# Layer 2's written-out block loop: stores and casts in later slots, refinement factors on ScalarE a block ahead, affine passes on GpSimd

## The chip, the core and the metric

The kernel runs on one core of a Trainium2 chip. A core has TensorE (PE, matrix products, transposes), VectorE (DVE), ScalarE (ACT) and GpSimd (POOL) for elementwise work, and SyncE (SP), which here only issues transfers. ScalarE issues transfers too, in its own instruction order. Each engine takes its instructions strictly as they stand in its queue, and waits on semaphores of the others. The metric is the device time of one execution in microseconds (us). The kernel before took 4350.38 us (median of three runs, 4346.45 to 4351.04).

## What is computed

Four graph layers over 4096 nodes with 256 features, each followed by a residual sum and a layernorm. Layers 0, 1 and 3 use the given 4096 x 4096 adjacency. The change lies in layer 2, which takes two steps of attention and diffusion:

```python
for n in range(2):
    A = top_p_attention(Xa, W1, W2, W3)      # rows of softmax, the largest kept up to 0.9 of the sum
    Xf = R @ Xf                              # R: adjacency plus identity, rows divided by their sum
    Xa = A @ Xa
    Z = Z + Xf @ U1[n].T + Xa @ U2[n].T
h = X + Z
x = layernorm(X + layernorm(h) * ln_g + ln_b)
```

The top-p cut of a row needs no full sort in the kernel. It guesses a cut, lists the largest elements below the guess, and finds the exact cut among these. In step 1 the guess is first made better by one Newton-like refinement.

## The kernel before, in words

Rows are worked in 32 blocks of 128 (NB = 32). For each step of layer 2 there is a preparation (keys, the first scores, a projection of all blocks) and then a loop over blocks b = 0..30, written out by hand with eight slots s = 0..7 in each block. Inside that loop the orders on PE, ACT, DVE and POOL are exactly the order in which the code calls them (`manual_schedule`). SyncE is not in that list: a planner orders its transfers, and may place one earlier in the queue than the slot in which the code asks for it.

In block b the slots hold, side by side, work for several blocks:

- **gather** (L1262): eight groups of products of the transposed, masked attention rows of block b with X, into the single buffer `ps_a`. Each group uses an `aT` that **turn** (L1253 transposes, L1255 ScalarE copy) made two slots earlier; the turns in slots 6 and 7 are already those of block b+1.
- **diffusion** (L175 load, L178 products) of block b+1, into the single buffer `ps_r`. It takes eight adjacency pieces of 256 KB from three `adj_piece` buffers, so piece p4 is loaded into the buffer of p1, and so on. In step 0 the slots hold 0,0,2,1,2,1,2,0 pieces, in step 1 0,0,2,1,2,2,1,0: in both, p4 is the first piece of slot 4.
- **scores** (L921, exponential L925) of block b+2 in slots 0 and 1.
- **guessed** for block b+2 on ScalarE in slots 2 to 7: a chain of 128x1 operations (helper `fma`, L934) around four 128x2048 passes (L1015). In slot 7 it ends with `c2`.
- **nucleus** for block b+1 on VectorE in slots 0 to 5: in slot 0 the cut `hi` (in step 1 after a full pass `S2` over the row, L941, and a chain of small operations, part of it on GpSimd, L1048 to L1053), in slots 1 and 2 a masked pass over half a row (L1070) and eight MAX8 (L1074) each, in slots 3 and 4 small operations, in slot 5 the mask passes over `e` (L1125).
- at the start of the block, **store** (step 0, L1358) or **closing** (step 1, L1365) of block b-1: ScalarE copies `ps_a` out as `h`. Only then may the next gather write `ps_a`.
- **diffused** (L1292): two VectorE passes that add the two halves of `ps_r` to `xb`. **base** (L1284/L1286) loads the next `xb` through SyncE, into one of two buffers.
- step 0: **keep** (slot 1): ScalarE casts `xb` (L126), VectorE subtracts (L127); the transfer out follows in slot 5.
- step 1: the rest of **closing**: first layernorm statistics in slot 1 (L85, L86 on VectorE, L88, L89 on GpSimd), the two affine passes on VectorE (L1370, L1371) and the second layernorm in slot 2 (L96 on GpSimd), the transfer of `h` out, issued by ScalarE, in slot 3 (L1374). **ahead3** turns and projects the `h` of two blocks before.

Of the kernel before, what the change touches and what calls it, by code (L numbers as in the profile page):

```python
# [23 lines left out]
P = 128  # L24
# [31 lines left out]
class Net:  # L56
# [684 lines left out]
    def layer2(self):  # L741
# [3 lines left out]
        with ExitStack() as ctx:  # L745
# [184 lines left out]
            def small(name, n=1, bufs=2):  # L930
                return work.tile([P, n], F32, name=name, bufs=bufs)
# [5 lines left out]
            def evaluate(name, e, c, bufs=2):  # L937
# [12 lines left out]
            def scores(b, q):  # L950

                zp = small("zp", HALF // 512)
                yield from product(q, es[b % 3][:, :N], sums=zp)
                zj = small("zj", HALF // 512)
                nc.scalar.activation(zj, zp, AF.Identity, accum_out=Zs[:, b:b + 1])

            def guessed(step, b):
# [26 lines left out]
                w = small("w", bufs=3)  # L984
                thr = small("cutoff", bufs=3)
                far = small("far", bufs=3)
                few = small("few")

                def rest(k):
# [34 lines left out]
                c2 = small("c2", bufs=3)  # L1024
                fma(c2, S1, ri, w)
                return c1, c2, S1, ri, thr, far

            def nucleus(step, b, c1, c2, S1, ri, thr, far):
# [9 lines left out]
                low, hi = small("low"), small("hi")  # L1038
                if step == 0:
                    nc.vector.tensor_scalar_mul(low, c1, 0.3)  # L1040
                    nc.vector.tensor_scalar(hi, c2, low, far, op0=ALU.max, op1=ALU.mult)
                else:
                    c, ic, gw, sq, d = (small(n) for n in ("c3", "ic", "gw", "sq", "d"))
# [7 lines left out]
                    nc.gpsimd.tensor_mul(gw, gw, ic)  # L1051
                    nc.gpsimd.tensor_scalar(sq, sq, 400.0, ri, op0=ALU.add, op1=ALU.mult)
                    nc.gpsimd.tensor_scalar_mul(low, c, 0.3)  # L1053
# [38 lines left out]
                nc.vector.tensor_copy(above[:, b:b + 1], bef[:, 0:1])  # L1092
# [35 lines left out]
            def mend(step, e, r):  # L1128
# [3 lines left out]
                with tc.If(nc.values_load(row[:, NB:], min_val=0, max_val=1) == 0):  # L1132
                    with tc.For_i(0, NB - 1, 1) as b:
                        with tc.If(nc.values_load(row[:, at(b)], min_val=0, max_val=1) == 0):
                            e2, Z = exact_scores(b)
                            r2 = exact_nucleus(e2, Z)
                            if step == 1:
                                xb = diffused(b, whole(diffusion(step, b)), base(step, b))
# [40 lines left out]
            def exact_scores(b, e=None):  # L1179
# [6 lines left out]
                nb = work.tile([P, 1], F32, name="nb")  # L1186
                nc.vector.tensor_reduce(nb, e, AX.X, ALU.max)
                nc.vector.tensor_scalar(nb, nb, -1.0, LOG_LIFT, op0=ALU.mult, op1=ALU.add)
                Z = work.tile([P, 1], F32, name="Z")
# [3 lines left out]
            def exact_nucleus(e, Z):  # L1193
# [7 lines left out]
                thr = work.tile([P, 1], F32, name="thr")  # L1201
# [4 lines left out]
                for bit in range(FREE_BITS - 1, -1, -1):  # L1206
                    S = work.tile([P, 1], F32, name="S")
                    nc.vector.scalar_tensor_tensor(junk, e, cand.bitcast(F32), e, op0=ALU.is_ge, op1=ALU.mult,
                                                   accum_out=S)
                    ok = work.tile([P, 1], I32, name="ok")  # L1210
# [8 lines left out]
                S = work.tile([P, 1], F32, name="S")  # L1219
                nc.vector.scalar_tensor_tensor(junk, e, tf, e, op0=ALU.is_gt, op1=ALU.mult, accum_out=S)  # L1220

                lim = work.tile([P, 2], F32, name="lim")
# [4 lines left out]
                sums = work.tile([P, N // CH], F32, name="sums")  # L1227
                before = -1.0
                for c in range(N // CH):
# [5 lines left out]
                    last = work.tile([P, 1], F32, name="last")  # L1235
# [6 lines left out]
                r = work.tile([P, 1], F32, name="r")  # L1242
# [118 lines left out]
            def closing(b, pa, r, xb):  # L1361
# [9 lines left out]
                nc.vector.scalar_tensor_tensor(hb, hb, rstd, xb[:, 1], op0=ALU.mult, op1=ALU.add)  # L1371
# [21 lines left out]
            for step in range(2):  # L1393
# [29 lines left out]
                with tc.manual_schedule(engines={ET.PE, ET.Activation, ET.DVE, ET.Pool}):  # L1423
                    for b in range(NB - 1):
# [6 lines left out]
                        for s in range(8):  # L1431
                            if s == 0:
# [6 lines left out]
                                bases[b] = diffused(b, pr, xb)  # L1439
# [25 lines left out]
                            if s == 5 and kept:  # L1465
# [25 lines left out]
                xb = diffused(b, pr, xb)  # L1491
# [127 lines left out]
```

## Time and profile before

| what | value |
|---|---|
| median of three runs | 4350.38 us |
| profiled execution | 4347.05 us, span of its instructions 4345.4 us |
| granted TensorE clock, mean | 0.975 |
| busy over the span | PE 92%, DVE 71%, ACT 61%, POOL 18% |
| loop of step 0 | from about 1820 to 2750 us; ScalarE's `h` (L1358) starts every 29.97 to 30.02 us |
| loop of step 1 | from about 2957 to 4045 us; ScalarE's `h` (L1365) starts every 34.9 to 35.4 us, mostly 34.98 |
| step 0, 2200 to 2300 us | PE 94.86, DVE 81.83, ACT 78.04, POOL 0.58 us busy in 100; clock 1.00 |
| step 1, 3250 to 3350 us | PE 90.67, DVE 90.00, ACT 68.98, POOL 34.52 us busy in 100; clock 0.98 |

The span is the time from the first to the last instruction; the profiled execution's own time is 1.65 us more. A timeline row gives the start, the length, engine, line, operation, and in brackets the idle time of that engine just before, with what ended it. A row of the waits gives who waited for whom, the total, the number of times and the longest. "PEld" is TensorE's weight load, which overlaps the products. "SPq" rows are transfers that SyncE issues. Times in text are from the start of the span.

### The profile page before, as it was taken

The page shows a single profiled execution, that of the slowest core. Times are in us where ns is not written, and L with a number is a line of the kernel's source. Part 1 is how long each engine was busy: PE and PEld are TensorE (multiplying, and loading weights), DVE is VectorE, ACT ScalarE, POOL GpSimd, SP SyncE. Part 2 cuts the span into 40 slices and gives each one's busy share as a digit, 9 for nine tenths or more (in the row PEclk, how much of TensorE's full clock was granted, in tenths as well). Part 3 has the DMA queues.
Part 4 walks back from the last instruction along what each step waited for, and adds up shares of the span by engine and source line. Part 5 has one row for each costly group of instructions (what it writes and reads, how often), then busy time and mean ns, then how long its engine had stood idle before and what let it go on. Part 6 is the DMA issues. An engine that isn't in the chain of part 4 may idle for free. (4 is left out here: it accounts for less than half of the span.)

```text
span 4345.4 us, 68954 instructions
## 1 busy us (share of the span) xinstructions
PE 3989.1 (92%) x25177; PEld 3402.9 (78%) x25177; DVE 3106.8 (71%) x7186; ACT 2651.1 (61%) x4695; POOL 796.9 (18%) x970
## 2 busy tenths in 40 slices
PE   7999989999997997899999999778999999999699
PEld 6899989999996884488888888636777777777587
DVE  7642349999994545477878778447999998999354
ACT  5533359999894224487877777245666666665232
POOL 0111111112430111100000000023333333333011
PEclk9999999999999999999999999999999999999899
DMA  4765562342223983322323323622222222222541
GB/s 126 228 200 176 179 233 80 103 156 80 65 71 137 361 313 77 114 88 92 97 89 95 94 87 97 203 65 90 89 88 87 84 84 85 88 85 86 188 132 48
DMA packets 301835, 537.03 MB, mean 124 GB/s; under 512 B 38310, under 2 KB 134310, under 8 KB 297382
## 3 DMA queue, kind: packets, MB, share of 16 engines
q1 hardware_dynamic: 209668, 379.80, 27.1%
q10 hardware_dynamic: 78946, 112.66, 7.5%
q0 software_dynamic: 12864, 39.99, 3.0%
q8 instruction: 203, 3.33, 0.3%
q14 instruction: 154, 1.26, 0.1%
HBM read 370.44 MB, written 161.87 MB: 123 GB/s over the span
## 5 line engine op out<-in xcount | busy, mean ns | idle before, releaser
L1262 PE MATMUL ps_a<-X,aT 128*128 128x256 f32 x4096 | 995.3, 387 | 88.4 <-ACT aT L1255 59.8
L1262 PEld LDWEIGHTS ps_a<-X,aT 128*128 128x128 f32 x4096 | 778.6, 193 | 237.4 <-ACT aT L1255 79.5
L299 PE MATMUL acc<-gm,gt 128*128 128x198 bf16 x8192 | 704.9, 249 | 25.8 <-issue 15.0
L299 PEld LDWEIGHTS <-gt 128*128 128x128 fp8e4 x8192 | 700.9, 97 | 29.9 <-issue 15.4
L291 ACT ACTIVATE sg<-lpb,nlc 128x1024 fp8e4<-128x1024 f32 x640 | 671.3, 1135 | 60.0 <-DVE gt L293 34.9
L178 PE MATMUL ps_r<-XD,adj_piece 128*128 128x512 f32 x2048 | 581.6, 418 | 5.9 <-DVE XD L127 4.5
L516 PE MATMUL pz<-src,ar 128*128 128x264 f32 x4096 | 509.7, 287 | 12.8 <-DVE ar L506 11.0
L516 PEld LDWEIGHTS pz<-src,ar 128*128 128x128 f32 x4096 | 506.7, 189 | 15.8 <-DVE ar L506 13.5
L1015 ACT ACTIVATE ja<-e,nc 128x2048 uint8<-128x2048 f32 x240 | 481.1, 2004 | 12.1 <-POOL h L96 8.8
L1255 ACT COPY aT<-ps_tp 128x512 f32<-128x512 f32 x512 | 296.3, 580 | 313.8 <-PE ps_tp L1253 293.7
L178 PEld LDWEIGHTS ps_r<-XD,adj_piece 128*128 128x128 f32 x2048 | 368.1, 191 | 86.2 <-issue 15.1
L1253 PE MATMUL ps_tp<-ident,e 128*128 128x128 f32 x2048 | 315.1, 278 | 60.2 <-DVE e L1125 44.1
L1253 PEld LDWEIGHTS ps_tp<-ident,e 128*128 128x128 f32 x2048 | 258.9, 144 | 126.9 <-issue 80.8
L1074 DVE MAX8 cand<-v 128x8 f32<-128x256 f32 x1024 | 347.2, 411 | 4.4
L1125 DVE SCALAR_TENSOR_TENSOR e<-e,edge 128x512 f32<-128x512 f32 x512 | 346.9, 750 | 2.2
L509 ACT ACTIVATE nb<-a 128x512 uint8<-128x512 f32 x256 | 156.4, 630 | 292.3 <-DMA a<-in_adjt_dram 280.4
L202 ACT ACTIVATE adj_piece<-na 128x1024 fp32r<-128x1024 fp8e4 x128 | 135.3, 1060 | 318.5 <-PE ps_adj L1525 91.9
L1070 DVE SCALAR_TENSOR_TENSOR v<-e,hi 128x2048 f32<-128x2048 f32 x128 | 299.0, 2336 | 1.2
L925 ACT ACTIVATE e<-ps_logit 128x1024 f32<-128x1024 f32 x256 | 259.8, 1022 | 42.3 <-PE ps_logit L921 27.6
L284 DVE TENSOR_SCALAR sg<-lpb,nlc 128x1024 fp8e4<-128x1024 f32 x384 | 282.7, 772 | 2.0
L921 PE MATMUL ps_logit<-kT,q 128*128 128x512 f32 x1024 | 276.5, 410 | 8.0 <-DVE kT L879 6.3
L88 POOL TENSOR_SCALAR ln_var<-ln_mv 128x1 f32<-128x1 f32 (+1 forms) x144 | 163.3, 1134 | 534.4 <-DVE ln_mv L86 497.0
(317 smaller groups left out, 5216.2 us busy)
## 6 DMA issues: line engine op xcount, KB each, us to landing
adj_piece<-adjs SPq DMA_DIRECT2D x512, 256.0 KB
a<-in_adjt_dram SPq DMA_DIRECT2D x256, 256.0 KB
adjs<-adj_piece SPq DMA_DIRECT2D x96, 512.0 KB
na<-nad SPq DMA_DIRECT2D x64, 512.0 KB
na<-nad ACTq DMA_DIRECT2D x32, 1024.0 KB
nad<-nb POOLq DMA_DIRECT2D x128, 128.0 KB, 3.3
lpb<-lpd POOLq DMA_DIRECT2D x32, 512.0 KB, 4.1
xfd<-part ACTq DMA_DIRECT2D x63, 256.0 KB
```

The costliest lines, as they stand in the source:

```text
L178: nc.tensor.matmul(ps, a[:, k, :], rhs(jc).rearrange("p s d -> p (s d)"), start=(jc == 0), stop=(jc == self.NB - 1))
L284: nc.vector.tensor_scalar(sg[:, k, :], lpb, nlc[:, jc, h:h + 1], 2.0 ** -5, op0=ALU.is_ge, op1=ALU.mult, saturate=False)
L291: nc.scalar.activation(sg[:, k, :], lpb, AF.Sign, scale=-1.0, bias=nlc[:, jc, h:h + 1], saturate=False)
L299: nc.tensor.matmul(acc[:, q, :6 * C1], gt[:, k, q * P:(q + 1) * P], gm[:, jc, hh, :], start=(jc == 0 and q % 2 == 0), stop=(jc == NB - 1 a ...
L516: nc.tensor.matmul(pz[q][:, t, :W], ar[:, q, k, :], src[:, jc, t, s], start=(jc == 0 and s == 0), stop=(jc == NB - 1 and s == 1))
L1015: nc.scalar.activation(ja, e[:, s * HALF:(s + 1) * HALF], f, bias=nc1, accum_out=fs[:, i + s:i + s + 1])
L1070: nc.vector.scalar_tensor_tensor(v, ec, hi, ec, op0=ALU.is_lt, op1=ALU.mult, accum_out=sb[:, s:s + 1])
L1074: nc.vector.max(cand[:, 8 * j:8 * j + 8], v[:, k * 256:(k + 1) * 256])
L1125: nc.vector.scalar_tensor_tensor(ec, ec, edge[:, j:j + 1], ec, op0=ALU.is_ge, op1=ALU.mult)
L1253: nc.tensor.transpose(pt[:, k * P:(k + 1) * P], e[:, jc * P:(jc + 1) * P], self.ident)
L1255: nc.scalar.copy(aT, pt)
L1262: nc.tensor.matmul(pa[:, :D], aT[:, k * P:(k + 1) * P], X[:, jc, :], start=(jc == 0), stop=(jc == NB - 1))
```

## The change

- `keep` (step 0): cast in slot 2, subtraction in slot 4, transfer in slot 6, in place of slots 1, 1 and 5.
- `diffused`: ScalarE scales the second half of `ps_r` into a new tile `dif` (one buffer), VectorE adds the first half to it in one pass, and GpSimd adds `dif` to `xb` after the first gather.
- `guessed` (step 1): what slot 0 of `nucleus` computed on VectorE and GpSimd (`c`, its reciprocal, `gw`, `sq`, the lower bound) is made by eleven ScalarE operations at the end of slot 7, a block ahead. The reciprocal is Ln and Exp. `w` is one ScalarE `fma` with `nthr`, not a multiplication and a GpSimd subtraction; `low` is made on ScalarE.
- `closing` (step 1): all of the first layernorm, with the affine multiplication and addition, on GpSimd in slot 1; the second layernorm in slot 3; the transfer of `h` in slot 7.
- `ahead3`'s transfers go from slot 5 to slot 6; the copy of `above` goes from VectorE to GpSimd.
- Most small tiles get one buffer in place of two; some per-block tiles two in place of three.

```diff
-            def small(name, n=1, bufs=2):
+            def small(name, n=1, bufs=1):
...
                     elif k == 1:
                         nc.scalar.mul(thr, Z, TOP_P)
-                        nc.scalar.mul(w, thr, ri)
-                        nc.gpsimd.tensor_sub(w, c1, w)
+                        nc.scalar.mul(nthr, Z, -TOP_P)
+                        fma(w, nthr, ri, c1)
+                        nc.scalar.mul(low, c1, 0.3)
...
                 fma(c2, S1, ri, w)
-                return c1, c2, S1, ri, thr, far
+                if step == 0:
+                    return c2, low, far, thr
+                c, gw, sq, lows = (small(n, bufs=2) for n in ("c3", "gw", "sq", "lows"))
+                ic = small("ic")
+                fma(c, low, -1.0, c2, AF.Relu)
+                fma(c, c, 1.0, low)
+                nc.scalar.activation(ic, c, AF.Ln)
+                nc.scalar.activation(ic, ic, AF.Exp, scale=-1.0)
+                fma(gw, S1, 1.0, nthr)
+                nc.scalar.mul(gw, gw, ic)
+                nc.scalar.activation(sq, gw, AF.Square)
+                nc.scalar.mul(gw, gw, ic)
+                fma(sq, sq, 1.0, cs[:, 11:12])
+                nc.scalar.mul(sq, sq, ri)
+                nc.scalar.mul(lows, c, 0.3)
+                return c, lows, far, thr, S1, gw, sq
...
                 if step == 0:
-                    nc.vector.tensor_scalar_mul(low, c1, 0.3)
-                    nc.vector.tensor_scalar(hi, c2, low, far, op0=ALU.max, op1=ALU.mult)
+                    nc.vector.tensor_scalar(hi, c, low, far, op0=ALU.max, op1=ALU.mult)
                 else:
-                    nc.vector.scalar_tensor_tensor(c, c1, 0.3, c2, op0=ALU.mult, op1=ALU.max)
-                    nc.vector.reciprocal(ic, c)
-                    nc.gpsimd.tensor_sub(gw, S1, thr)
-                    nc.gpsimd.tensor_mul(gw, gw, ic)
-                    nc.gpsimd.tensor_mul(sq, gw, gw)
-                    nc.gpsimd.tensor_mul(gw, gw, ic)
-                    nc.gpsimd.tensor_scalar(sq, sq, 400.0, ri, op0=ALU.add, op1=ALU.mult)
-                    nc.gpsimd.tensor_scalar_mul(low, c, 0.3)
                     S2 = evaluate("S2", e, c)
...
-                nc.vector.tensor_copy(above[:, b:b + 1], bef[:, 0:1])
+                nc.gpsimd.tensor_copy(above[:, b:b + 1], bef[:, 0:1])
...
             def diffused(b, pr, xb):
-                for part in (slice(0, D), slice(D, 2 * D)):
-                    nc.vector.scalar_tensor_tensor(xb[:, 0], pr[:, part], rdeg[:, at(b)], xb[:, 0],
-                                                   op0=ALU.mult, op1=ALU.add)
+                dif = work.tile([P, D], F32, name="dif", bufs=1)
+                nc.scalar.mul(dif, pr[:, D:], rdeg[:, at(b)])
+                nc.vector.scalar_tensor_tensor(dif, pr[:, :D], rdeg[:, at(b)], dif, op0=ALU.mult, op1=ALU.add)
+                yield
+                nc.gpsimd.tensor_add(xb[:, 0], xb[:, 0], dif)
                 return xb
...
-                self.split(part, xb[:, 0])
+                nc.scalar.copy(part[:, 0], xb[:, 0])
+                yield
+                nc.vector.tensor_sub(part[:, 1], xb[:, 0], part[:, 0].bitcast(F32))
                 yield
                 nc.scalar.dma_start(xfd[b], part.bitcast(F32))
...
                 nc.gpsimd.tensor_add(hb, hb, xb[:, 0])
                 yield
-                mv, rstd = self.moments(work, h)
+                self.layernorm(work, h, h, nc.gpsimd)
+                nc.gpsimd.tensor_mul(hb, hb, affine)
+                nc.gpsimd.tensor_add(hb, hb, xb[:, 1])
                 yield
-                nc.vector.scalar_tensor_tensor(hb, hb, mv[:, 0, 0:1], affine, op0=ALU.subtract, op1=ALU.mult)
-                nc.vector.scalar_tensor_tensor(hb, hb, rstd, xb[:, 1], op0=ALU.mult, op1=ALU.add)
                 self.layernorm(work, h, h, nc.gpsimd)
...
-                                bases[b] = diffused(b, pr, xb)
+                                difs = diffused(b, pr, xb)
+                                next(difs)
...
                             gather(pa, aTs.pop(0), s)
-                            if s in (1, 2, 3) and close:
+                            if s == 0:
+                                bases[b] = result(difs)
+                            if s in (1, 3, 7) and close:
                                 v = result(close)
-                                if s == 3:
+                                if s == 7:
                                     done[b - 1] = v
-                            if s == 1 and step == 0:
-                                kept = keep(b, bases.pop(b))
-                                next(kept)
+                            if step == 0:
+                                if s == 2:
+                                    kept = keep(b, bases.pop(b))
+                                if s in (2, 4, 6):
+                                    result(kept)
...
-                            if s == 5 and kept:
+                            if s == 6 and step == 1 and kept:
                                 whole(kept)
```

More of the change, by code (lines that the diff above doesn't have):

```diff
@@ L950, in scores @@
             def scores(b, q):
-                zp = small("zp", HALF // 512)
+                zp = small("zp", HALF // 512, bufs=2)
                 yield from product(q, es[b % 3][:, :N], sums=zp)
@@ L983, in guessed @@
                 ri = small("ri", bufs=3)
-                w = small("w", bufs=3)
+                w = small("w", bufs=2)
                 thr = small("cutoff", bufs=3)
+                nthr = small("nthr")
+                low = small("low", bufs=2)
                 far = small("far", bufs=3)
@@ L1200, in exact_nucleus @@
                 CH = 1024
-                thr = work.tile([P, 1], F32, name="thr")
+                thr = work.tile([P, 1], F32, name="thr", bufs=1)
                 nc.vector.tensor_scalar_mul(thr, Z, TOP_P)
@@ L1226, in exact_nucleus @@
                 nc.vector.tensor_scalar_mul(lim[:, 1:2], tf, -1.0)
-                sums = work.tile([P, N // CH], F32, name="sums")
+                sums = work.tile([P, N // CH], F32, name="sums", bufs=1)
                 before = -1.0
@@ L1234, in exact_nucleus @@
                     nc.vector.tensor_tensor_scan(cnt, ones.to_broadcast([P, CH]), eq, before, op0=ALU.mult, op1=ALU.add)
-                    last = work.tile([P, 1], F32, name="last")
+                    last = work.tile([P, 1], F32, name="last", bufs=1)
                     nc.vector.tensor_copy(last, cnt[:, CH - 1:CH])
@@ L1241, in exact_nucleus @@
                                                    accum_out=sums[:, c:c + 1])
-                r = work.tile([P, 1], F32, name="r")
+                r = work.tile([P, 1], F32, name="r", bufs=1)
                 nc.vector.tensor_reduce(r, sums, AX.X, ALU.add)
@@ L1490, in layer2 @@
                         finish(k, done.pop(k))
-                xb = diffused(b, pr, xb)
+                xb = whole(diffused(b, pr, xb))
                 if step == 0:
```

24 lines of the change are left out of this document (12 added, 12 removed).

## The prediction

> **What bounds the kernel now.** The change touches the two loops of layer 2, so I read the waits of each loop's window, then the instruction timeline of one steady block, then short stretches with busy time and clock.
>
> The waits of step 0's loop (1820 to 2780 us):
>
> ```profile
> DVE part L127 <- ACT part L126: 134.7, 30, 4.7
> PE ps_tp L1253 <- DVE e L1125: 38.5, 30, 1.3
> ```
>
> TensorE works through each 29.98 us block but for 1.28 us, when it waits for VectorE's first mask pass. VectorE is late because it stood 4.5 us behind ScalarE's cast. So TensorE alone would need 28.7 us.
>
> The waits of step 1's loop (2980 to 4050):
>
> ```profile
> POOL h L1366 <- ACT h L1365: 285.1, 31, 13.0
> ACT part L126 <- POOL h L96: 195.4, 25, 7.8
> ...
> DVE d L1055 <- POOL gw L1051: 45.8, 30, 1.6
> PEld ps_a L1262 <- ACT h L1365: 38.7, 29, 3.4
> ```
>
> VectorE's only real wait is 1.58 us: it bounds the 34.98 us block. ScalarE stands up to 7.8 us, and TensorE waits for it at each block's first gather.
>
> One block of step 1, rows of the timeline (all engines; rows between left out):
>
> ```profile
> 3301.13 0.47 ACT L1365 ACTIVATE h<-ps_a,inv 128x256 f32<-128x256 f32 x1
> ...
> 3301.68 4.45 POOL L1366 TENSOR_TENSOR h<-h,xb 128x256 f32<-128x256 f32 x1 [9.05 <-ACT h L1365]
> ...
> 3309.29 2.32 DVE L1070 SCALAR_TENSOR_TENSOR v<-e,hi 128x2048 f32<-128x2048 f32 x1
> 3309.30 1.27 SPq L175 DMA_DIRECT2D adj_piece<-adjs  x2
> 3309.46 2.23 POOL L88 TENSOR_SCALAR ln_var<-ln_mv 128x1 f32<-128x1 f32 x1 [1.65 <-DVE ln_mv L86]
> ...
> 3311.77 0.57 POOL L89 TENSOR_TENSOR ln_rstd<-ln_var,power 128x1 f32<-128x1 f32 x1
> ...
> 3314.85 0.48 DVE L1371 SCALAR_TENSOR_TENSOR h<-h,ln_rstd,xb 128x256 f32<-128x256 f32 x1
> ...
> 3315.36 0.33 SPq L1286 DMA_DIRECT2D xb<-xd  x1
> ...
> 3315.79 12.89 SPq L175 DMA_DIRECT2D adj_piece<-adjs  x6
> ...
> 3316.95 2.12 PE L178 MATMUL ps_r<-XD,adj_piece 128*128 128x512 f32 x8
> ...
> 3319.08 1.25 POOL L96 TENSOR_SCALAR h<-h,ln_mv,ln_rstd 128x256 f32<-128x256 f32 x1
> ```
>
> GpSimd's L88, 0.22 us when alone, ends just after VectorE's masked pass: a tensor pass of VectorE and one of GpSimd exclude each other. SyncE issues the `xb` load right behind L1371, the last reader of that buffer, and only then p6, whose buffer was free earlier: the load holds the queue.
>
> Short stretches: DMA share and GB/s are the last two columns, the clock stands before them.
>
> ```profile
> 3317.80:3318.20 0.40, 0.40 (x4) 0.32 (x3) 0.40 (x2) 0.00 (x0) 0.40 (x1) 1.00 0.88 338
> 3318.20:3318.90 0.70, 0.70 (x5) 0.56 (x4) 0.67 (x4) 0.00 (x0) 0.62 (x2) 1.00 0.02 6
> 3218.00:3221.41 3.41, 1.50 (x7) 1.24 (x7) 3.06 (x16) 3.38 (x6) 0.00 (x0) 1.00 0.53 154
> 3221.41:3224.82 3.41, 3.41 (x11) 2.75 (x11) 2.99 (x16) 3.27 (x6) 0.19 (x1) 0.50 0.32 115
> ```
>
> The `xb` load and p6, issued from 3315.36 on, are through by 3318.2: 2.85 us after the first issue. A 3.41 us stretch in which TensorE idles 1.9 us is followed by one at half clock.
>
> **Step 0.** The cast in slot 2 and the subtraction in slot 4 have their inputs long before: the 4.5 us stall goes. VectorE also loses one L1292 (0.48) and `low` (0.14). It then masks some 4 us before TensorE asks, and the 1.28 us wait ends: 30 x 1.28 = 38.4 us gained. ScalarE gets `dif` (0.47, as L1365), `nthr` and `low` (0.2 each); they lie in its waits for transposes (0.35 to 2.4 us a slot). GpSimd's `xb` addition (0.72 alone, under 3 behind a masked pass) is due 5 us later. SyncE's queue in the changed program holds, per block, q, p4, p5, p6, xb, p7, p8 and the next three pieces; the xb load now waits for the subtraction in slot 4. From the start H of ScalarE's `h`: VectorE gets there at H+16.1 to 16.6, p7 lands by H+20, TensorE wants it at H+21.5. Covered, with 1.5 us to spare. Bounds of the gain: 30 to 40 us.
>
> **Step 1, what VectorE loses.** L1044/L1045 0.28, the wait 1.58, one L1292 0.50, L1370/L1371 1.09, the copy of `above` 0.07, the wait at L127 0.2: 3.7 us, leaving 31.3. TensorE's rows of the block without their waits come to 30.6. If that were all, the block would take 31.3 us. Two things take its place.
>
> **First, ScalarE's new chain is on the path.** The eleven operations stand between the copy of slot 6's turn and that of slot 7; then come `h` and `dif`. TensorE's first gather waits for `h`, and VectorE's first pass of the block for `dif`. None of these starts before slot 6's turn. From that turn's start: copy of `aT` +0.66, first `n` +0.48, the five old operations 1.76 (3333.88 to 3335.63), the new ones, `aT` 0.46. The new ones: seven of the form of `n` or `ri` (0.29, 0.33 start to start), four of the short form (0.19 to 0.20, 0.22 to 0.23): 3.2 us. Bounds: 11 x 0.22 = 2.4 and 11 x 0.42 = 4.6; the named rows are nearest. So H of the next block is slot 6's turn + 6.6 us.
>
> **Second, the xb load moves ahead of p4.** In the changed program SyncE's queue in step 1 is, per block, q, xb, p4 to p8, next three; before, p4 and p5 stood ahead of xb. The last reader of that `xb` is now GpSimd's last affine addition, no longer L1371. When is it done?
>
> - ScalarE's next operation starts 0.37 after `h`, and `dif` is 0.47 long: at H+0.87 VectorE starts its pass on it (0.5), then S2 (4.5), the small chain (1.62), statistics (0.55): the first masked pass starts at H+8.0. GpSimd's `xb` addition, shut out by S2, runs when it ends and may hold the small chain 0.6 us: H+8.0 to 8.65.
> - From that start, GpSimd: variance done at 2.40, L89 at 3.05, L96 at 3.16 to 4.41, the multiplication at 4.48 to 5.20 (0.72, as the unblocked additions). VectorE's second masked pass is due at 4.99. The multiplication is in, so the pass starts at 5.2; the addition, ready at 5.27, must wait for its end at 7.5: done at 8.2. Bounds for the two operations: 1.5 us (neither blocked) and 5 us (both); the due times say one.
> - The xb load goes out at H+16.25 to 16.85, p4 lands 2.9 later, H+19.15 to 19.75. TensorE wants it at H+15.82 (3316.95 less 3301.13). It stands 3.3 to 3.9 us. Behind it stand the products of slots 4, 5 and 6.
>
> From p4 to slot 6's turn TensorE has five pieces (0.98 each), three gathers (1.73) and two turns (0.36), 10.8 us: H+30.0 to 30.55. VectorE's first mask is there by H+27.8 to 28.4 (26.0 us of its own rows after the `dif` pass begins, and 0.9 from 3329.43 and 2204.12, mask starts, to the turn): no longer the last. With 6.7 the next H comes after 36.7 to 37.2. The first gather's wait grows from some 1.5 to 2.7 us, p4's is over 3.3: by the stretches above both bring half-clock stretches, each worth up to 1.7 us. The first only shortens the wait for p4; the second counts in about half the blocks: +0.9. I take 37.7 us; bounds 36.5 (no slow stretch, chain unhindered) and 38.95 (every block).
>
> [...]
>
> **Sum.** Step 0: -38.4. Step 1: 28 steady blocks x (37.7 - 34.98) = +76, the first two intervals (31.5 and 33.4 before, closing not yet full) +4.5. Tail: the last `closing` has L96, multiplication and addition (1.35 + 0.79 + 0.79) in place of L1371 (0.5), on the chain that ends last: +2.4. The one-buffer tiles cost nothing: writer and readers are one engine, or a block apart. The moved transfers cost nothing either: `keep`'s leaves in slot 6, its tile is written again in the next slot 2; `closing`'s stands in slot 7 on ScalarE, some 10 us after GpSimd's last pass, and `h` is overwritten in the next slot 3; `ahead3`'s are one slot later. If that cover were gone, each would stop ScalarE's chain for its 0.34 us or more. The copy of `above` is 128x1 on GpSimd, in a free place. ScalarE no longer waits 7.8 us for L96; that is lost in waits for TensorE. 4347.05 - 38.4 + 76 + 4.5 + 2.4 = 4391.5; the runs' median stands 3.3 above the profiled execution: 4395.
>
> **Rivals.** Changes under 0.2% (8.7 us) are about what a measurement cannot tell from none.
>
> - *As summed, 4395; its own range 4362 to 4430.* 0.67.
> - *The addition slips in before the second masked pass* (it misses by 0.3 us), or the load comes sooner. Then p4 lands at H+17 to 17.5, TensorE stands about 1.2 us, and slot 6's turn (H+27.8 to 28.3) and the chain give 34.4 to 35.0 us: 4294 to 4312, plus 3. For: two rows decide it by 0.3 us. Against: before, the variance fell behind the masked pass in every block. 0.16.
> - *The change does what VectorE's sum says*, chain and load hidden: 31.3 us, 4347 - 38.4 + 2.4 - 29 x 3.7 = 4204. Against: ScalarE's order leaves `h` behind the chain. 0.04.
> - *Both in part:* 35.9 to 36.3 us a block, 4341 to 4353. The sign turns at 36.1 us, where step 1's loss eats 38.4. 0.08.
> - *Step 0 gains nothing too* (p7 late behind xb by over 1.5 us): 4433. 0.05.
>
> Faster 0.16 + 0.04 + 0.01, slower 0.67 + 0.05 + 0.01, same 0.06. Range 4300 to 4432: it leaves out the gain in full, part of the early addition, and the very top.
>
> **What the changed profile would show.** Right: in step 0 no wait of L1253 for the mask, a block of 28.7 us; in step 1 TensorE waiting over 2.5 us for `adj_piece` in every block, SyncE waiting for GpSimd at the xb load, VectorE waiting about 5 us for `dif`, ScalarE's chain running unbroken before `h`, half-clock stretches more often. Wrong: p4 there in time, or the xb load out before H+14. What would make it wrong is most of all the place of one 0.72 us addition.

## The result and the profile after

The changed kernel takes 4376.24 us (median of 4 executions, 4371.94 to 4382.05), the kernel before 4349.41 us beside it: ratio 1.0063, 95% interval 1.0046 to 1.0081. It is slower by 27 us. The profiled execution of after took 4375.62 us, with a span of 4373.9 us and a mean granted clock of 0.970 (before: 0.975).

Where the time went, from the two profiled executions. Marks are starts of ScalarE's copies: the first `xb` of the projection, then the `h` of each loop.

| stretch | before, us | after, us | difference | predicted |
|---|---|---|---|---|
| start to step 0's projection | 1711.69 | 1708.54 | -3.2 | 0 |
| projection, to step 0's first `h` | 136.90 | 127.30 | -9.6 | 0 |
| 30 blocks of step 0 | 895.92 | 852.92 | -43.0 | -38.4 |
| to step 1's first `h` | 241.44 | 239.57 | -1.9 | 0 |
| 30 blocks of step 1 | 1043.53 | 1130.52 | +87.0 | +80.5 |
| the rest | 315.87 | 315.01 | -0.9 | +2.4 |
| span | 4345.35 | 4373.85 | +28.5 | +44.5 |

Both loops went as forecast in sign and nearly in size: step 0 gained more, step 1 lost more, and the projection gained what had been put at nothing.

The waits of step 0's loop after the change (1820 to 2740 us; who waited for whom, total, times, longest):

```profile
ACT aT L1264 <- PE ps_tp L1262: 110.5, 157, 5.3
DVE dif L1302 <- ACT dif L1301: 106.1, 30, 3.6
```

TensorE's wait for the first mask pass is no longer in the list. VectorE now waits 3.5 us a block for `dif`, and ScalarE for TensorE, which has no idle row left in a steady block: TensorE alone sets the block, 28.49 us from `h` to `h` (29.98 before).

The waits of step 1's loop after the change (2920 to 4060 us):

```profile
DVE dif L1302 <- ACT dif L1301: 242.8, 30, 57.4
...
ACT h L1397 <- DVE part L127: 139.7, 29, 5.9
...
PE ps_r L178 <- DMA adj_piece<-adjs: 79.9, 44, 3.7
...
PE ps_a L1271 <- ACT h L1378: 70.7, 30, 4.1
```

VectorE's `dif` wait, TensorE's waits for the pieces and its wait for `h` had been named. The second row had not: ScalarE stands some 4.8 us in each block behind VectorE's L127, in slot 3.

SyncE's own queue in step 1 (2960 to 4000 us):

```profile
SPq L1295 <- POOL h L1383: 274.5, 27, 23.8
```

The `xb` load (L1295) waits for GpSimd's last affine addition in nearly every block, with p4 and all later pieces behind it. One block, rows of the timeline of all engines (rows between left out):

```profile
3304.91 0.47 ACT L1378 ACTIVATE h<-ps_a,inv 128x256 f32<-128x256 f32 x1
...
3306.18 4.47 DVE L941 SCALAR_TENSOR_TENSOR v<-e,c 128x4096 bf16<-128x4096 f32 x1
3306.34 4.90 POOL L1304 TENSOR_TENSOR xb<-xb,dif 128x256 f32<-128x256 f32 x1
...
3317.56 0.74 POOL L1382 TENSOR_TENSOR h<-h,affine 128x256 f32<-128x256 f32 x1
...
3317.90 0.37 ACT L126 CAST part<-ps_logit 128x256 fp32r<-128x256 f32 x1 [1.13 <-PE ps_logit L1343]
3318.18 2.35 DVE L1079 SCALAR_TENSOR_TENSOR v<-e,hi 128x2048 f32<-128x2048 f32 x1
3318.38 2.74 POOL L1383 TENSOR_TENSOR h<-h,xb 128x256 f32<-128x256 f32 x1
...
3321.14 0.34 SPq L1295 DMA_DIRECT2D xb<-xd  x1
3321.57 13.89 SPq L175 DMA_DIRECT2D adj_piece<-adjs  x8
...
3323.75 0.41 DVE L127 TENSOR_TENSOR part<-ps_logit,part 128x256 fp32r<-128x256 f32 x1
...
3324.19 0.37 ACT L1397 COPY h<-ps_logit 128x256 f32<-128x256 f32 x1 [5.92 <-DVE part L127]
...
3324.59 3.40 PE L178 MATMUL ps_r<-XD,adj_piece 128*128 128x512 f32 x8 [3.64 <-DMA adj_piece<-adjs]
...
3334.22 0.59 ACT L1264 COPY aT<-ps_tp 128x512 f32<-128x512 f32 x1 [0.93 <-PE ps_tp L1262]
...
3339.90 0.29 ACT L934 ACTIVATE c<-low,c 128x1 f32<-128x1 f32 x1
...
3342.57 0.56 ACT L1264 COPY aT<-ps_tp 128x512 f32<-128x512 f32 x1
...
3343.04 0.48 ACT L1378 ACTIVATE h<-ps_a,inv 128x256 f32<-128x256 f32 x1
```

With H = 3304.91: the multiplication (L1382) is in before VectorE's second masked pass, the addition (L1383) starts 0.2 us behind that pass and is shut out, 2.74 us long. The load goes out at H+16.23, p4 starts at H+19.68 after a wait of 3.64 us, the next `h` stands at H+38.13. All of this is in the prediction, which has 37.7 for the last. Beside it lies the row that is not: L1397 comes at H+19.28, after 5.92 us of standing, and from there to the next `h` ScalarE has 18.85 us with only 1.2 us idle in it, 0.93 of them at 3334.22, where it waits for TensorE's turn of slot 5. Two paths of nearly the same length end in this `h`: one by p4 and TensorE, one by L127 and ScalarE's own rows. In 16 of the 27 steady blocks ScalarE's last wait of 0.4 us or more ahead of the next `h` is for the turn of slot 5, in 9 it is for L127.

### The profile page after: what moved, and what is told of

It reads as the page before. It is cut to its first block, busy times and chain, and to the rows that moved or that the text cites. A ratio compares the mean times of both kernels' runs of the same rounds, so it can differ in the third digit from the quotient of the medians.

```text
span 4373.9 us, 69004 instructions
## 1 busy us (share of the span) xinstructions
PE 4003.4 (92%) x25177; PEld 3424.3 (78%) x25177; DVE 3056.0 (70%) x6898; ACT 2778.1 (64%) x5239; POOL 900.4 (21%) x938
## 5 line engine op out<-in xcount | busy, mean ns | idle before, releaser
L178 PE MATMUL ps_r<-XD,adj_piece 128*128 128x512 f32 x2048 | 595.6, 425 | 87.0 <-DMA adj_piece<-adjs 81.5
L1018 ACT ACTIVATE ja<-e,nc 128x2048 uint8<-128x2048 f32 x240 | 481.1, 2004 | 10.2 <-issue 8.7
L1079 DVE SCALAR_TENSOR_TENSOR v<-e,hi 128x2048 f32<-128x2048 f32 x128 | 312.2, 2439 | 3.3
L921 PE MATMUL ps_logit<-kT,q 128*128 128x512 f32 x1024 | 289.5, 424 | 11.5 <-DVE kT L879 6.4
L1302 DVE SCALAR_TENSOR_TENSOR dif<-ps_r,rdeg,dif 128x256 f32<-128x256 f32 x64 | 30.9, 484 | 351.3 <-ACT dif L1301 351.3
```

The costliest lines, as they stand in the source:

```text
L178: nc.tensor.matmul(ps, a[:, k, :], rhs(jc).rearrange("p s d -> p (s d)"), start=(jc == 0), stop=(jc == self.NB - 1))
L921: nc.tensor.matmul(pl[:, s, :], q[:, t, :], kT[:, (2 * c + s) * 512:(2 * c + s + 1) * 512], start=(t == 0), stop=(t == 1))
L1018: nc.scalar.activation(ja, e[:, s * HALF:(s + 1) * HALF], f, bias=nc1, accum_out=fs[:, i + s:i + s + 1])
L1079: nc.vector.scalar_tensor_tensor(v, ec, hi, ec, op0=ALU.is_lt, op1=ALU.mult, accum_out=sb[:, s:s + 1])
```

## The experiments

Block times are means from `h` to `h` in step 1, over some 27 steady blocks of the profiled execution. The changed kernel's is 38.04 us, the kernel before's 34.99. Where SyncE's order is left to the planner, an edit elsewhere can move the `xb` load in it; this happened in experiments 2 and 5, and is said there.

**1. The load out of the way.** SyncE's order is left to the code in step 1, and the load is written into slot 6.

```diff
-with tc.manual_schedule(engines={ET.PE, ET.Activation, ET.DVE, ET.Pool}):
+with tc.manual_schedule(engines={ET.PE, ET.Activation, ET.DVE, ET.Pool} | ({ET.SP} if step == 1 else set())):
...
-                            if s == 4:
+                            if s == (4 if step == 0 else 6):
                                 xb = base(step, b + 1)
```

> The changed kernel with one thing different: in step 1 SyncE's transfers are issued in the order written, and the xb load is written into slot 6, so that it stands behind p8 and no longer ahead of p4. Theory (the load ahead of p4, together with ScalarE's chain, makes the block): p4 is there in time, TensorE no longer waits for adj_piece, VectorE's mask bounds the turn of slot 6 at H+27.8 to 28.3, ScalarE's chain of 6.6 us follows: 34.4 to 35.0 us a block in place of 38.0, whole kernel 4270 to 4290 us. Rival 1 (the load is harmless; the chain or GpSimd's passes set the block): 37.5 to 38 us a block, 4365 to 4380. Rival 2 (the chain is hidden, the load does all the harm): 31.3 us a block, about 4175.

Measured: 4346.14 us (ratio 0.999 to before, 0.998 to 1.0), 36.78 us a block. TensorE's wait for pieces is gone from the list, but the block is shorter by only 1.3 us, not by 3.0 to 3.6. All three expectations fail. ScalarE's rows of one block of this kernel (timeline):

```profile
3294.30 0.47 ACT L1378 ACTIVATE h<-ps_a,inv 128x256 f32<-128x256 f32 x1
...
3313.59 0.37 ACT L1397 COPY h<-ps_logit 128x256 f32<-128x256 f32 x1 [3.04 <-DVE part L127]
...
3331.08 0.47 ACT L1378 ACTIVATE h<-ps_a,inv 128x256 f32<-128x256 f32 x1
```

ScalarE gets to the copy at H+19.29, when VectorE has done L127, and then works 17.49 us without one idle row: 36.78. VectorE for its part has no wait between `dif`, which follows `h`, and L127. This is a second path, and it is the limit as soon as the load is not.

**2. The chain away.** The factors are made as before, on VectorE and GpSimd in slot 0.

```diff
-                c, gw, sq, lows = (small(n, bufs=2) for n in ("c3", "gw", "sq", "lows"))
...
-                nc.scalar.mul(lows, c, 0.3)
-                return c, lows, far, thr, S1, gw, sq
+                return c2, low, far, thr, S1, ri
...
-                    d = small("d")
+                    c, ic, gw, sq, d, lows = (small(n, bufs=2) for n in ("c3", "ic", "gw", "sq", "d", "lows"))
+                    nc.vector.tensor_tensor(c, c2, low, ALU.max)
+                    nc.vector.reciprocal(ic, c)
+                    nc.gpsimd.tensor_sub(gw, S1, thr)
...
+                    nc.gpsimd.tensor_scalar_mul(lows, c, 0.3)
```

> The changed kernel with the refinement factors made as before, in slot 0 on VectorE (maximum, reciprocal) and GpSimd (six small operations); ScalarE's eleven operations of slot 7 are gone, all else is as changed. Theory: 3.2 us less between the turn of slot 6 and H, but GpSimd's small operations now stand behind its xb addition and VectorE waits for them, so the first masked pass, GpSimd's last addition, the xb load and p4 come 1.5 to 2.5 us later: 36.0 to 36.8 us a block, 4310 to 4345 us. Rival 1 (the chain alone costs, the load is harmless): 34.8 us, about 4283. Rival 2 (the load alone costs, the chain is hidden): 38 us and over, 4376 or more.

Measured: 4312.53 us (ratio 0.991, 0.9893 to 0.9926), 35.29 us a block: the time lies in the theory's range, the block between its 36.0 and the first rival's 34.8. But more than the chain is changed here. The planner put the `xb` load behind p4 and p5, as in the kernel before, and TensorE waits for p6 instead of p4. SyncE's and ScalarE's rows of one block:

```profile
3289.58 0.47 ACT L1369 ACTIVATE h<-ps_a,inv 128x256 f32<-128x256 f32 x1
...
3297.74 1.26 SPq L175 DMA_DIRECT2D adj_piece<-adjs  x2
...
3307.18 0.33 SPq L1286 DMA_DIRECT2D xb<-xd  x1
...
3310.21 0.37 ACT L1388 COPY h<-ps_logit 128x256 f32<-128x256 f32 x1 [7.27 <-DVE part L127]
...
3324.86 0.47 ACT L1369 ACTIVATE h<-ps_a,inv 128x256 f32<-128x256 f32 x1
```

The same path as in 1: 20.63 us to L127 (VectorE is 1.3 us later, with its part of the factors and 0.9 us of waiting for `gw`), then 14.65 us of ScalarE's rows without an idle one, 2.84 less without the chain. So the run shows that ScalarE's path is the limit here too. What the load costs it does not show.

**3. Step 0 alone.** The kernel before, with `keep` in slots 2, 4 and 6.

```diff
-                self.split(part, xb[:, 0])
+                nc.scalar.copy(part[:, 0], xb[:, 0])
+                yield
+                nc.vector.tensor_sub(part[:, 1], xb[:, 0], part[:, 0].bitcast(F32))
...
-                            if s == 1 and step == 0:
-                                kept = keep(b, bases.pop(b))
-                                next(kept)
+                            if step == 0:
+                                if s == 2:
+                                    kept = keep(b, bases.pop(b))
+                                if s in (2, 4, 6):
+                                    result(kept)
...
-                            if s == 5 and kept:
+                            if s == 5 and step == 1 and kept:
```

> The kernel before with one part of the change: in step 0 the cast, the subtraction and the transfer of keep stand in slots 2, 4 and 6. Theory (the gain of step 0 is the end of VectorE's stand behind ScalarE's cast): step 0's block goes from 29.98 to 28.5 us, step 1's stays 34.98, whole kernel 4300 to 4310. Rival 1 (the gain needs the shorter diffused pass of VectorE as well): the block stays over 29.2, 4325 to 4350. Rival 2 (the projection stage's 8 us belong to it too): 4295 or less.

Measured: 4304.56 us (ratio 0.9886, 0.987 to 0.9903), as the theory has it; 30 blocks of step 0 in 854.63 us (895.92 before, 852.92 in the changed kernel), step 1 unchanged at 34.99. The place of the cast and the subtraction brings 41.3 of the 43.0 us of step 0; the new `diffused` is not needed for them. The projection takes 106.2 us here from its first to its last `xb` copy, as before (107.0); in the changed kernel it is 98.8: that gain does not belong to `keep`.

**4. The addition before the masked pass.** GpSimd's multiplication is left out.

```diff
                 self.layernorm(work, h, h, nc.gpsimd)
-                nc.gpsimd.tensor_mul(hb, hb, affine)
                 nc.gpsimd.tensor_add(hb, hb, xb[:, 1])
```

> The changed kernel without GpSimd's multiplication by the layernorm's scale in closing (it leaves out that multiplication in step 1 and in the tail). Theory: the last affine addition starts before VectorE's second masked pass and not behind it, so it ends some 3 us earlier, the xb load goes out at H+13.3 to 13.9, p4 lands 3.4 later and TensorE waits for it 1 to 1.5 us at most: 34.5 to 35.2 us a block, 4275 to 4300 us. Rival 1 (the load is harmless): at most the 0.7 us of the operation a block, 4354 to 4376. Rival 2 (the addition is shut out all the same, by L96 falling late): under 1 us a block, 4350 to 4376.

Measured: 4344.66 us (ratio 0.9982, 0.9973 to 0.9992), 36.77 us a block. Timeline of one block:

```profile
3297.26 0.47 ACT L1378 ACTIVATE h<-ps_a,inv 128x256 f32<-128x256 f32 x1
...
3309.93 0.73 POOL L1382 TENSOR_TENSOR h<-h,xb 128x256 f32<-128x256 f32 x1
3310.55 2.35 DVE L1079 SCALAR_TENSOR_TENSOR v<-e,hi 128x2048 f32<-128x2048 f32 x1
3310.69 0.33 SPq L1295 DMA_DIRECT2D xb<-xd  x1
...
3316.55 0.37 ACT L1396 COPY h<-ps_logit 128x256 f32<-128x256 f32 x1 [4.28 <-DVE part L127]
...
3334.01 0.47 ACT L1378 ACTIVATE h<-ps_a,inv 128x256 f32<-128x256 f32 x1
```

The theory's first half holds: the addition slips in, 0.73 us long in place of 2.74, and the load goes out at H+13.4 as forecast. The block still takes what ScalarE's path takes, here 19.29 + 17.46 = 36.75: in the mean the same 36.8 as with the load moved. So the prediction's rival "the addition slips in early" had its place right and its price wrong.

**5. ScalarE's stand, and the load one place later.** `ahead3` copies `h` before the cast, so that it is not behind L127. The load was meant to stay ahead of p4, but the planner placed it behind p4 and ahead of p5.

```diff
                     part = work.tile([P, 2, D], F32R, name="part", bufs=1)
+                    nc.scalar.copy(h[:, 0], pz[:, :D])
                     self.split(part, pz[:, D:])
-                nc.scalar.copy(h[:, 0], pz[:, :D])
+                if last:
+                    nc.scalar.copy(h[:, 0], pz[:, :D])
```

> The changed kernel with one thing different: ahead3 copies ScalarE's h out of PSUM before the cast and VectorE's subtraction (L127), not behind them, so that ScalarE no longer stands in slot 3 until VectorE reaches L127. New theory (two paths of nearly the same length: the load path by p4, and ScalarE's rows, 17.5 us without a pause from the copy behind L127 to the next h; the load path alone): p4 still lands at H+19.7, slot 6's turn follows 10.8 later and h 6.6 after it: 37.1 to 37.9 us a block, 4345 to 4375 us. Rival (ScalarE's path alone sets the block, the load is cover only): 34.4 to 35.0 us a block, 4270 to 4290.

Measured: 4370.75 us (ratio 1.005, 1.0033 to 1.0067), 37.55 us a block, inside the theory's 37.1 to 37.9, though by another piece. SyncE's and TensorE's rows of one block, whose `h` is at 3495.96:

```profile
3504.13 0.34 SPq L175 DMA_DIRECT2D adj_piece<-adjs  x1
...
3511.76 1.18 PE L178 MATMUL ps_r<-XD,adj_piece 128*128 128x512 f32 x4
...
3512.20 0.33 SPq L1295 DMA_DIRECT2D xb<-xd  x1
...
3515.74 2.07 PE L178 MATMUL ps_r<-XD,adj_piece 128*128 128x512 f32 x4 [2.80 <-DMA adj_piece<-adjs]
```

p4 goes out at H+8.17 and is there in time; p5 goes out behind the load, and TensorE waits for it, here until H+19.78; it is p5 in each of the 27 steady blocks. So the 0.5 us a block that this run gains cannot be put down to ScalarE's stand, and the interval of its time overlaps with the changed kernel's (1.0046 to 1.0081). Experiment 9 has the stand alone. The waits (2960 to 3900 us) no longer hold L127 as a releaser of ScalarE; what stays is the load path:

```profile
PE ps_r L178 <- DMA adj_piece<-adjs: 66.0, 25, 3.7
...
PE ps_a L1271 <- ACT h L1378: 58.2, 25, 3.4
```

**6. Both.** Edits 1 and 5 together.

> The changed kernel with both: SyncE's transfers in step 1 in the order written, the xb load behind p8, and ahead3's copy of h before the cast. New theory (two paths, both now gone): VectorE's mask and the turn of slot 6 at H+27.8 to 28.3, ScalarE's chain of 6.6 behind it: 34.4 to 35.0 us a block, 4270 to 4290 us. Rival 1 (ScalarE's sum of work holds it all the same): 36 us and over, 4320 or more. Rival 2 (the chain is hidden once ScalarE is early): 31.3 to 32 us, 4175 to 4200.

Measured: 4273.17 us (ratio 0.9824, 0.9807 to 0.984), 34.10 us a block (34.05 in most): the time is in the theory's range, the block 0.3 us under it. The load's place alone was worth 1.3 us a block (1), the copy's place alone nothing (9); together they are worth 3.9. Two paths in parallel, each close behind the other, is what that means. TensorE's remaining waits in this kernel (2960 to 3900 us) are those for `h`, behind the chain, and for the mask:

```profile
PE ps_a L1271 <- ACT h L1378: 56.5, 28, 2.3
...
PE ps_tp L1262 <- DVE e L1134: 31.9, 26, 2.7
```

**7. The chain behind `h`.** As 6; `c` is made behind `h` and `dif`, the other nine operations behind the two exponentials of slot 0. `factors` holds the eleven operations of the change unaltered, with a `yield` behind the first two; `nthr` has a second buffer.

```diff
+            def factors(c2, low, far, thr, S1, ri, nthr):
...
                                 next(difs)
+                                if step == 1:
+                                    facts = factors(*guess)
+                                    next(facts)
...
+                            if s == 0:
+                                if step == 1:
+                                    guess = whole(facts)
+                                edge = nucleus(step, b + 1, *guess)
```

> As the kernel with both (load behind p8, copy of h before the cast), and ScalarE's eleven operations no longer stand between the turns of slots 6 and 7 and h: c (two operations) is made behind h and dif, the other nine behind the two exponentials of slot 0. Theory (the chain's place on the way to h costs its 3.2 us): slot 6's turn at H+28.0 to 28.6, h 3.4 later: 31.4 to 32.2 us a block, 4175 to 4205 us. Rival (chain hidden, or its length now held against VectorE's d, which needs gw at H+6): 33.5 us and over, 4240 or more.

Measured: 4203.16 us (ratio 0.9665, 0.9649 to 0.9682), 31.69 us a block, both in the theory's ranges. The chain stood on the path with 2.4 us. This version beats both kernels, by 3.4% and 4.0%. Two blocks of it, busy time of PE, PEld, DVE, ACT and POOL, then the clock, DMA share and GB/s:

```profile
3062.09:3125.45 63.36, 61.29 (x301) 50.35 (x300) 60.36 (x157) 51.98 (x128) 31.64 (x22) 1.00 0.31 96
```

TensorE is busy 61.3 of 63.4 us, at full clock, and the timeline shows no wait of VectorE in a block: VectorE is the limit now. The prediction had 31.3 us for this case, from VectorE's rows.

**8. The factors on VectorE and GpSimd again.** As 6, with edit 2.

> As the kernel with both (load behind p8, copy of h before the cast), and the refinement factors made as before on VectorE and GpSimd in slot 0. Theory: VectorE's row is 0.3 us longer and waits 0.9 us for GpSimd's gw, so its mask is 1.2 us later than with the factors on ScalarE, and h follows slot 6's turn by 3.4: 32.4 to 33.2 us a block, 4205 to 4235 us. Rival (VectorE's wait for gw grows because GpSimd's xb addition is shut out): 34 us and over, 4255 or more.

Measured: 4263.07 us (ratio 0.9802, 0.9786 to 0.9819), 33.77 us a block. The range is missed, and the time is in the rival's; but not for the rival's reason, since VectorE waits 0.9 us for `gw`, as the theory has it. Blocks have about two lengths, 32.6 us (inside the range) and 34.3. The mask starts 28.37 us after `h` in both (0.3 later where VectorE still had the last block's mask to finish). The difference is the clock. Three adjoining stretches of 3.41 us at the end of a long block, and two at the end of the short one that follows (columns as above):

```profile
3095.62:3099.03 3.41, 1.45 (x8) 0.97 (x7) 3.10 (x13) 2.21 (x4) 0.00 (x0) 1.00 0.53 152
3099.04:3102.45 3.41, 3.41 (x11) 2.87 (x11) 3.41 (x6) 2.14 (x6) 0.00 (x0) 0.50 0.11 38
3102.46:3105.87 3.41, 3.41 (x18) 2.87 (x18) 2.00 (x6) 2.44 (x6) 1.26 (x2) 1.00 0.00 0
...
3129.76:3133.17 3.41, 1.46 (x7) 0.97 (x6) 3.09 (x13) 2.35 (x4) 0.00 (x0) 1.00 0.60 166
3133.17:3136.58 3.41, 3.40 (x20) 3.02 (x21) 3.41 (x6) 2.60 (x8) 0.00 (x0) 1.00 0.11 38
```

TensorE idles 1.96 us, waiting for the mask, which starts 28.4 us after `h` here and 27.5 us after it in 7; the next stretch runs at half clock, and the block is 1.7 us longer. In the short block TensorE idles as long, 1.95 us of it in one stretch, and the next stretch is at full clock. What decided between two stretches so nearly alike the trace does not show.

**9. The load's place.** As 6, but the load is written ahead of p4 again, in SyncE's written order.

```diff
+                            if s == 4:
+                                xb = base(step, b + 1)
                             for _ in range(pieces[s]):
                                 next(beside)
...
-                            if s == (4 if step == 0 else 6):
-                                xb = base(step, b + 1)
```

> As the kernel with both (SyncE's transfers in step 1 in the order written, ahead3's copy of h before the cast), but the xb load is written ahead of p4 again, where the changed kernel's planner had put it. Theory (the load's place ahead of p4 is what costs, not who orders the queue): as with the copy alone, 37.1 to 37.9 us a block, 4345 to 4375 us. Rival (something else in the written order, q's place for instance, made the gain): 34.1 us a block, 4265 to 4280.

Measured: 4383.61 us (ratio 1.0079, 1.0059 to 1.0099), 38.04 us a block: just above the theory's range, and far from the rival's 34.1. The place of this one transfer costs 3.9 us a block, with the queue in the written order both times. This is also the changed kernel's load path without ScalarE's stand: TensorE waits for p4 in each of the 27 blocks, ScalarE no longer for L127, and the block is as long as the changed kernel's. There the stand costs nothing that shows. (2960 to 3900 us:)

```profile
PE ps_r L178 <- DMA adj_piece<-adjs: 67.6, 31, 4.0
```

**10. The affine passes back on VectorE.** As 7, with that part of the change undone.

```diff
-                self.layernorm(work, h, h, nc.gpsimd)
-                nc.gpsimd.tensor_mul(hb, hb, affine)
-                nc.gpsimd.tensor_add(hb, hb, xb[:, 1])
+                mv, rstd = self.moments(work, h)
                 yield
+                nc.vector.scalar_tensor_tensor(hb, hb, mv[:, 0, 0:1], affine, op0=ALU.subtract, op1=ALU.mult)
+                nc.vector.scalar_tensor_tensor(hb, hb, rstd, xb[:, 1], op0=ALU.mult, op1=ALU.add)
                 self.layernorm(work, h, h, nc.gpsimd)
```

> The fastest kernel so far (31.69 us a block: load behind p8, copy before the cast, ScalarE's factors behind h) with one part of the change undone: the first layernorm's affine passes are again two VectorE passes (in slot 3), not three GpSimd passes in slot 1. Theory (VectorE now bounds the block, it has no waits left): 1.09 us more a block, less what VectorE loses to GpSimd's passes now: 32.3 to 32.8 us a block, 4220 to 4240 us. Rival (VectorE is not the bound, or loses as much to GpSimd's passes): 31.5 to 31.8 us, 4195 to 4207.

Measured: 4256.61 us (ratio 0.9792, 0.9769 to 0.9815), 33.66 us a block, both above the theory's: there are blocks of 32.6 us, as the theory has them, and of 34.3, as in 8. TensorE's wait for the mask, 31.4 us in 29 blocks in 7, is here (both 2960 to 3900 us):

```profile
PE ps_tp L1263 <- DVE e L1135: 57.9, 28, 3.5
```

0.9 us more of VectorE's work cost 2.0 us a block. With the load and the chain placed well, this part of the change is worth 53 us.

**11. The projection.** GpSimd's subtraction for `w` is back for the two blocks ahead of each loop.

```diff
-                        fma(w, nthr, ri, c1)
+                        if b < 2:
+                            nc.scalar.mul(w, thr, ri)
+                            nc.gpsimd.tensor_sub(w, c1, w)
+                        else:
+                            fma(w, nthr, ri, c1)
```

> The changed kernel with GpSimd's subtraction for w put back for blocks 0 and 1 of each step, which are made ahead of the loop; the loops are as changed. Theory (the projection stage of step 0 became shorter because GpSimd's xb additions no longer stand in its queue behind this subtraction, which waited 69.5 us for ScalarE): the projection takes 105 to 107 us again in place of 99 to 101.5, whole kernel 4 to 9 us longer than the changed one, 4380 to 4385 us. Rival (it came from the planner's new order or the buffers): 99 to 101.5 us, 4370 to 4379.

Measured: 4391.31 us in the median (4376.60 to 4392.98), but the projection takes 100.9 us, not 105 to 107. GpSimd stands behind this subtraction again (waits of the projection, 1713 to 1815 us):

```profile
POOL w L1000 <- ACT w L999: 74.0, 2, 69.2
```

and nobody pays for it: the theory falls. In the other experiments built on the changed kernel the projection takes 99.0 to 101.5 us. The extra 15 us of the whole lie elsewhere, 7 of them in step 1's loop (1137.4 us against 1130.5), whose blocks scatter from 37.1 to 40.2 us; the edit does not touch those blocks. Between programs with the load ahead of p4, 0.3 us a block (38.33 in the mean here, 38.04 in the changed kernel) is therefore not to be read as an effect. What shortened the projection, the planner's new order or the buffers, is left open.

## Why the prediction was right, and where it was not

The sign and the mechanism of step 1 were right: 27 us slower, 45 forecast.

- **Step 0** was mis-sized: 43.0 us gained in 30 blocks, not 38.4, and outside the bounds of 30 to 40. The term "30 x 1.28" took the wait's row for the whole of what a wait costs TensorE; the block became shorter by 1.49 us, 0.2 more than the row. Experiment 3 shows that `keep` alone brings 41.3 of it. The load was covered there, as forecast.
- **"What VectorE loses", 31.3 us.** Experiment 7 gives 31.69 when VectorE alone is the limit. The working was right; as forecast, it was not what decided the changed kernel.
- **The chain on the path** was right in place and 0.5 us too long: 3339.90 to 3342.57 in the block shown, 2.67 us for the forecast 3.2, and 2.4 us a block when it is moved (6 against 7).
- **The load ahead of p4.** The addition misses the second masked pass as forecast (the forecast had 0.3 us, the trace 0.2), the load goes out at H+16.23 (16.25 to 16.85), p4 starts at H+19.68 (19.15 to 19.75); the landing took 3.45 us, not 2.9. Over the 27 steady blocks the terms add up in the mean: p4's products start at H+19.73, slot 6's turn follows 11.86 us later (forecast 10.8, and 0.9 for the clock), `h` 6.45 us after that (6.6): 38.04. The load path without ScalarE's stand gives 38.04 us as well (experiment 9), for a forecast of 37.7. The path runs by one turn earlier than forecast: ScalarE's last wait for TensorE is at slot 5's turn (in 16 of the 27 blocks, and in all 27 of experiment 9), and from that copy its rows take 8.8 to 8.9 us to `h`.
- **One step was wrong and did not count here:** the sentence that ScalarE's 7.8 us behind L96 are "lost in waits for TensorE". They were not: ScalarE stands behind VectorE's L127 in place of L96, 4.8 us a block, and then has 17.5 us of unbroken rows. This path alone gives 36.78 us (experiment 1), 1.3 us less than the load path, so the changed kernel's block does not show it. It makes one rival's price wrong: "the addition slips in early" was to give 4294 to 4312 us, and experiment 4 gives 4345. The forecast held because the addition was shut out, by 0.2 us.
- **Half-clock stretches** were to count in about half the blocks, at up to 1.7 us: 0.9. The clock rows of the changed kernel show 34 in 30 blocks of step 1 (16 before, where they cost nothing, since VectorE bounded the block). In 12 of the 27 steady blocks one falls between the start of p4's products and slot 6's turn and costs 1.4 to 1.7 us there, 0.7 in the mean. In the other 15 it falls ahead of p4, where it only shortens the wait for it (mostly 1.8 to 2.1 us in place of 3.5 to 3.7), as forecast. This term was right. Most of the rest lies within the products of p4 and p5, which take 2.3 to 2.9 us in place of 2.1 where the clock is full.
- **The other stages** have no term in the sum; the projection's 9.6 us are the largest reason why the forecast was too high. Its cause is open (experiment 11). "Tail +2.4" is not to be seen in the rest's -0.9.

The cast, L127 and L1397 all read one `ps_logit` tile, and the row [5.92 <-DVE part L127] has L1397 start at 3324.19, right behind L127 (3323.75 + 0.41). Why a copy that only reads the tile stands behind another reader no run shows; written ahead of the cast, in experiments 5 and 9, it no longer waits for L127.

## What to carry to other kernels

Before an engine's stall is called harmless, add up its rows from the end of the stall to the point where others wait for it: a long unbroken run of rows is a path, even on an engine that has long idle times elsewhere. Removing one of two nearly equal paths shows little or nothing (1.3 and 0 us a block), removing both shows 3.9, so a small effect does not refute a cause. And when the work of a tile moves to a later engine, look up in the issuing queue what stands behind the transfer that reuses the tile: here one load's place cost 3.9 us a block. Look it up again in the trace of every variant where a planner orders that queue: experiments 2 and 5 did not touch the load, and it moved.

## What the runs showed of the hardware

- In experiment 8 a stretch of 3.41 us in which TensorE idled 1.96 us was followed by one at half clock, and one with 1.95 us by one at full clock; the one with 1.91 us in the prediction's rows was followed by half clock. The idle time of one stretch alone does not sort them. The price came out whole: blocks of 32.6 and 34.3 us stand side by side in experiments 8 and 10, with equal marks up to the mask. In experiment 7, with waits of 1.0 us, no half-clock stretch falls into step 1's 30 blocks; in 8 there are 20, in 10 there are 17. So this loop has a step in its cost: 0.9 us of later work cost 2.0.
- GpSimd's 128x256 addition takes 0.73 us alone, 2.74 behind VectorE's half-row pass and 4.90 behind its full-row pass (L1304 above): in both cases it ends 0.6 us after VectorE's pass. 0.2 us of lateness cost 2.0. VectorE's L1064, beside the end of L1304, takes 0.56 us and ends with it; the same operation takes 0.22 us in the kernel before (L1055), with no addition beside it. So the prediction's "exclude each other" is shown for these passes, not for all: beside VectorE's MAX8 rows GpSimd's multiplication (L1382) takes 0.73 us, as alone.
- ScalarE's queue keeps its order also where a later row is ready: in the block shown, L1018 has its last input, `nc`, from 3314.62 on, and starts at 3324.46, behind L1397 at 3324.19.
